# A two-layer graph network on one Trainium2 core: gathers ahead of a norm's root, means in place, one row by TensorE, two updates later

## The chip, the core and the metric

The kernel runs on one core of a Trainium2 chip. A core has five engines with an instruction queue each: TensorE (PE: matrix products and transposes; PEld is its weight load), VectorE (DVE), ScalarE (ACT), GpSimd (POOL) and SyncE (SP), which issues transfers. Sixteen DMA engines move the data. Each queue runs in its own order, and an instruction whose operands aren't ready holds up everything behind it on its engine. The metric is the device time of one execution in microseconds (us), as the median of several runs.

## The reference

There are 16 graphs of 1024 nodes with 256 features each, and one adjacency shared by all of them. Two layers are computed, each added to its input:

```python
def _gat(inp, adj_mask, W, a):
    h = jnp.matmul(inp, W)
    f1 = jnp.matmul(h, a[:F_, 0])
    f2 = jnp.matmul(h, a[F_:, 0])
    e = jax.nn.leaky_relu(f1[:, :, None] + f2[:, None, :], ALPHA)
    if adj_mask is not None:
        e = jnp.where(adj_mask[None, :, :] > 0, e, NEG_INF)
    att = jax.nn.softmax(e, axis=2)
    return jax.nn.elu(jnp.einsum('bij,bjf->bif', att, h))
...
h = jnp.maximum(_layernorm(x, axis=-1), 0.0)
out = jax.nn.relu(jnp.matmul(h, mlp1_w) + mlp1_b)       # 256 -> 512
out = jax.nn.elu(_gat(out, None, W_fc, a_fc)) + out     # dense attention
out = jax.nn.relu(jnp.matmul(out, mlp2_w) + mlp2_b)     # 512 -> 256
out = jax.nn.elu(_gat(out, adj, W_hand, a_hand)) + out  # masked attention
x = x + jax.nn.relu(out)
h = jnp.maximum(_layernorm(x, axis=-1), 0.0)
x = x + <masked attention of h with W, a, slope 0.01, relu in place of elu>
```

## The kernel before

**Tiles and stages.** A graph's nodes are cut into 8 tiles of 128 (two halves of four). For each graph the kernel goes through these stages: the first norm (`Norm`, name `0`), mlp1, dense attention (`Dense`), mlp2, the first masked attention (`Gnn0`, tensors `hma`, `atta`, `oa`), the second norm (`Norm`, name `1`), the second masked attention (`Gnn1`, `hmb`, `attb`, `ob`) and the store. The stages of neighbouring graphs are interleaved, so that a graph's masked attentions run while the next graph's dense attention is prepared.

**Dense attention without a dense product.** A softmax weight of the dense attention depends on a node only through one number. The kernel therefore ranks the nodes by that number (`rank`, L516 to L523), scatters their rows in sorted order to a table in memory (`scatter`, L530), reads the table back (`read_sorted`, L574), and forms running sums from both ends (`sum_before`, `sum_behind`, L602 to L617). It writes these to a fine table (sums within blocks of 8 rows, L609) and a coarse one (sums over blocks, `carry`, L631). `sign` (L553, on ScalarE, one pass over 1024 numbers for each tile) counts each node's place; `gather` (L642, GpSimd) fetches the fine row at that place and then adds the coarse one; `share` (L654 to L657, VectorE) works out the denominators, and `mean` (L664 on ScalarE, L666 on VectorE) makes a tile's mean, called `hp`. `merge` (L713 to L717) transposes four `hp` tiles and takes the elu; `merge_end` (L723 on VectorE, L724 on GpSimd) adds it to `resT`, which mlp2 (L731) reads.

**Graph 0 is different.** It is `split`: its first half goes through a plain product (`weight`, `product`, `product_mean`, L687 to L706), while only its second half goes through the tables. Its gathered tiles have the tag `hm`. An `hp` tile has a pool of four buffers, shared by the halves.

**The order of the work.** It is written out by hand. `at(lo, hi, steps)` puts steps into a table with due times in nominal microseconds. The table is sorted by due time, and each step issues its instructions in that order onto all queues that it uses. For TensorE, VectorE, ScalarE and SP this order is binding; on GpSimd it is enforced with dependencies, with scatters free among themselves. Due times only make an order: an engine runs ahead or behind as its operands allow. Graph b's own base is at `b * 142 - 28` (0 for graph 0), and the opening is counted from `START = -168`. A due time of -61.2 in the opening comes at about 122 us of the trace, and 0 at about 184.

**The masked attentions.** `row` needs one number of each node along the free axis, in all partitions. For graphs in `AHEAD` (1 to 14) `send` transposes the numbers, copies them and writes them to memory from ScalarE's queue (L243 to L246), and `row(True)` reads them back to all partitions from SP's queue (L360). For graphs 0 and 15 `row()` makes eight transposes of a broadcast column on TensorE (L238) and two copies on ScalarE (L365). `weight` (L375) then makes an `att` tile on VectorE, in a ring of 8 buffers, and `product` (L385) uses it. `finish`, `combine` (ScalarE, then two adds on GpSimd, L413 and L414) and `update` (L418, VectorE) end a tile; `stats` (L262, L263) and `root` (L267, L268, GpSimd) prepare the second norm; `center` (L272) and `turn` (L282) transpose it for the next projection.

Around the update, GpSimd's order in a steady graph is: adds of tiles 4 and 5, four fine gathers of the next graph's first half, the norm's first root, adds of tiles 6 and 7, four more fine gathers, two coarse ones, the norm's second root, the other coarse ones.

Of the kernel before, what the change touches and what calls it, by code (L numbers as in the profile page):

```python
# [8 lines left out]
F32 = mybir.dt.float32  # L9
# [8 lines left out]
P = 128  # L18
# [13 lines left out]
def fast_path(ctx: ExitStack, tc: tile.TileContext, alarm, x, adj, w1, b1, w2, b2, w_fc, a_fc,  # L32
# [24 lines left out]
    NT = N // P  # L57
# [3 lines left out]
    TH = HALF // P  # L61
    R = H + 2
    K = H + 1
# [3 lines left out]
    work = ctx.enter_context(tc.tile_pool(name="work", bufs=2))  # L67
# [154 lines left out]
    def at(lo, hi, steps):  # L222
        for i, step in enumerate(steps):
            table.append((lo + (hi - lo) * i / len(steps), len(table), step))
# [212 lines left out]
    class Dense:  # L437
# [221 lines left out]
        def mean(self, h, u):  # L659
            n = TH // len(self.got[h])  # L660
            got, den = self.got[h][u // n][:, u % n, :], self.dens[h]
            name = f"{self.b}_{h}_{u}"
            part = work.tile([P, K], F32, tag="part", name=f"part_{name}")
            nc.scalar.activation(part, got[:, :K], AF.Copy, scale=den[:, 1, u:u + 1])  # L664
            hp = self.hps[h, u] = work.tile([P, K], F32, tag="hp", name=f"hp_{name}", bufs=TH)
            nc.vector.scalar_tensor_tensor(hp, got[:, K:], den[:, 0, u:u + 1], part,  # L666
                                           op0=OP.mult, op1=OP.add)

# [86 lines left out]
    xs = {}  # L755
# [17 lines left out]
    def each(f, *ranges):  # L773
        out = [()]
        for r in ranges:
            out = [o + (i,) for o in out for i in r]
        return [partial(f, *o) for o in out]

    def first_norm(t0, b):

        n = norm1[b]
        lo = t0 - (62 if b == 2 else 33.5)
        at(lo, lo + 1, n.stats_steps(0))
        at(t0 - 13, t0 - 9, n.stats_steps(1))
        n.turn_at(t0 - (14.5 if b == 2 else 22), 0, 4 if b == 2 else 7)
        n.turn_at(t0 + 0.2, 1, 4)
# [49 lines left out]
    def gathers(d, h, lo, hi):  # L836
        at(lo, lo + 4, each(d.gather, [h], [0], range(TH)))
        at(hi, hi + 7, each(d.gather, [h], [1], range(TH)))
# [20 lines left out]
    def merges(lo, d, h):  # L859
        at(lo, lo + 9.2, each(d.merge, [h], range(HC)))  # L860
        at(lo + 2.5, lo + 11.7, each(d.merge_end, [h], range(HC)))

    def second_mlp(t0, b, after=0):
        d, m = dense[b], gnn0[b]
        for i, lo in enumerate((102.5, 104.8, 113, 116.5)):
            lo += t0 - 3.4 * last(b)
            at(lo, lo, [partial(d.mlp2, i // FC, i % FC)])
        t0 += after
        at(t0 + 135, t0 + 142, each(m.project, range(NT)))
        at(t0 + 141.9, t0 + 141.9, [m.extremes])  # L870

    def weights(m, t, n, lo, hi):
        at(lo, hi, each(m.weight, [t], [n], range(NT)))

    def masked_first(t0, b):
        m, n = gnn0[b], norm2[b]
        at(t0 + 1, t0 + 1, [m.vectors])
        lo = t0 + 11
        if b in AHEAD:
            at(t0 + 3.4, t0 + 3.4, [m.send])  # L880
            at(t0 + 6, t0 + 6, [partial(m.row, True)])
            lo += 7
        else:
            at(t0 + 4, t0 + 4, [m.row])
        at(t0 + 4.5, lo - 1, each(m.scale, range(NT)))
        weights(m, 0, 2, lo - 5.5, lo - 1)
        at(t0 + 10, t0 + 10, [partial(load_again, b)])
        if last(b, 2):
            for q, start in enumerate((0.5, 2, 4.2, 5.5)):
                at(t0 + start, t0 + start, [partial(dense[b].natural, q)])  # L890
        else:
            at(t0 + 4.5, t0 + 11, each(dense[b].natural, range(NT // 2)))
        pairs = [(t, 2) for t in range(0, NT, 2)]
        if last(b):
            pairs[-1:] = [(NT - 2, 1), (NT - 1, 1)]
        for t, n_t in pairs:
            start = lo + 3.5 * t
            at(start, start + 3.5 * n_t, each(m.product, [t], [n_t], range(NT)))
            if t:
                weights(m, t, n_t, start - 5.5, start + 1)  # L900
        for t in range(NT):
            end = lo + 7.2 + 7 * (t // 2) + 0.6 * (t % 2)
            if last(b) and t == NT - 2:
                end -= 3.5
            at(end, end, [partial(m.finish, t)])
            at(end + 1.2, end + 1.2, [lambda t=t: m.combine(t, dense[b].o_nat)])
            if last(b) and t >= NT - 2:
                at(end + 2.6, end + 2.6, [lambda t=t: m.add(t, dense[b].o_nat, nc.vector)])
                end -= 2
            at(end + 5.2, end + 5.2, [lambda t=t: m.update(t, xs[b])])  # L910
            end += 5.6 if last(b) else 6.2 if b == 0 else 9
            at(end, end, [partial(n.stats, t)])
        at(lo + 25 - 3.4 * last(b), lo + 25 - 3.4 * last(b), [partial(n.root, 0)])
        lo += 33.1 if last(b) else 35.5 if b == 0 else 38.5
        at(lo, lo, [partial(n.root, 1)])

    def last(b, n=1):
        return b >= NB - n
# [58 lines left out]
    AHEAD = range(1, NB - 1)  # L977
# [4 lines left out]
    START = -168.0  # L982
    n, d = norm1[0], dense[0]
# [34 lines left out]
    for t in range(TH):  # L1018
        lo = START + 95 + 7.1 * t
        at(lo, lo + 7, each(d.product, [t], range(NT)))  # L1020
        at(lo + 8.2, lo + 8.2, [partial(d.product_mean, t)])
    at(START + 100, START + 107, each(d.weight, [1], range(NT)))
    gathers(d, 1, START + 108, START + 114)
    e = dense[1]
    at(START + 95.5, START + 95.5, [e.columns])
    at(START + 98.5, START + 98.5, [e.row, e.highest])
    at(START + 99, START + 118, each(e.rank, range(NT)))
    at(START + 118, START + 118, [less_columns])
    merges(START + 125, d, 0)
    at(START + 135, START + 135, [partial(d.share, 1)])  # L1030
    at(START + 135.5, START + 137, each(d.mean, [1], range(TH)))
    merges(START + 138.2, d, 1)
    second_mlp(START + 39, 0, -13)
    at(START + 123.4, START + 141, each(e.project, range(NT), [0]))
    scatters(e, START + 126, START + 142)
# [1 line left out]
    at(START + 142.5, START + 142.5, [e.read_sorted])  # L1037
    at(START + 76, START + 76, [partial(load_first, 2)])
    first_norm(0, 2)
    at(START + 147, START + 147, [e.sums_begin])  # L1040
    at(START + 144, START + 158, each(e.sign, range(NT)))
    for h in range(2):
        at(START + 150 + 3 * h, START + 150 + 3 * h, [partial(e.sums_weights, h)])
        at(START + 151 + 5 * h, START + 156 + 5 * h, each(e.sum_before, tiles(h)))
# [6 lines left out]
    for b in range(NB):  # L1051
        base, after_base = base_of(b), base_of(b + 1)
        masked_first(base, b)
        second_norm(base, b)
        pairs = range(0, NT, 2)
# [25 lines left out]
        if b + 3 < NB:  # L1081
            lo = after_base - PERIOD + 86
            at(lo, lo, [partial(load_first, b + 3)])
            first_norm(after_base, b + 3)
# [433 lines left out]
def two_layer_gat(tc, *args):  # L1518
    nc = tc.nc
    with tc.tile_pool(name="alarm", bufs=1) as pool:  # L1520
        alarm = pool.tile([1, 1], I32, name="alarm")
        fast_path(tc, alarm, *args)
        with tc.If(nc.values_load(alarm[0:1, 0:1], min_val=0, max_val=1,
                                  skip_runtime_bounds_check_because="it is 0 or 1") > 0):
            general_path(tc, *args)
# [24 lines left out]
```

## Time and profile before

| | us |
|---|---|
| median of 3 runs (lowest, highest) | 2355.42 (2349.34, 2355.79) |
| the profiled execution | 2359.75 |
| its span, first to last instruction | 2357.9 |
| TensorE busy | 2268.6 (96%) |
| VectorE busy | 1625.7 (69%) |
| ScalarE busy | 1241.3 (53%) |
| GpSimd busy | 951.4 (40%) |
| GpSimd idle before L267 (root), waiting for VectorE | 148.4, 48.0 of it at once |
| VectorE idle before L418 (update), waiting for GpSimd | 55.5, in 14 waits |
| VectorE idle before L375, waiting for the row's transfer | 11.5, in 10 waits |

A timeline line has the start, the duration, the engine, the source line, the operation, what it writes and reads, its shape and count, and in brackets the engine's idle time before it with the instruction that ended it. A group of lines that follow one another is merged. The number of a wait says what an engine lost; whether the kernel lost it too depends on what stood behind.

### The profile page before, as it was taken

The numbers are of one execution on the slowest core, as the hardware profiler recorded it, in microseconds if no ns is written. First come the engines' busy times: TensorE is split into PE (matmuls) and PEld (weight loads), VectorE is DVE, ScalarE is ACT, GpSimd is POOL, SyncE is SP. The second block draws the span as 40 slices with busy tenths as digits, with TensorE's granted clock in tenths as the row PEclk, the third lists the DMA queues.
The fourth block names the chain that finished last, engine by engine and source line by source line (L and its number), as shares of the span: only waits on it lengthen the run. The fifth ranks groups of instructions, "written<-read, shape, count | busy, mean of one in ns | idle before, by whom it ended". The sixth has DMA issues, their size and how long they took to land. (4 is left out here: it accounts for less than half of the span.)

```text
span 2357.9 us, 30868 instructions
## 1 busy us (share of the span) xinstructions
PE 2268.6 (96%) x9955; PEld 1747.4 (74%) x9955; DVE 1625.7 (69%) x4535; ACT 1241.3 (53%) x2744; POOL 951.4 (40%) x1212
## 2 busy tenths in 40 slices
PE   8989999999999999999999999999999999999888
PEld 6667787777878778786776877777786876877666
DVE  6666685866858567685866867576685856767655
ACT  5345655647365463745546374554736546373442
POOL 1153435354443536334263543526444353533420
PEclk9999999999999999999999999999999999999999
DMA  4658366572656747366573745657265673737500
GB/s 173 165 159 210 72 176 165 167 193 97 200 118 175 180 143 184 97 187 161 172 187 113 186 115 165 174 161 181 91 195 143 174 184 125 185 95 182 140 21 27
DMA packets 150874, 355.81 MB, mean 151 GB/s; under 512 B 11224, under 2 KB 62760, under 8 KB 146608
## 3 DMA queue, kind: packets, MB, share of 16 engines
q1 hardware_dynamic: 104080, 189.58, 28.8%
q0 software_dynamic: 45952, 163.99, 26.3%
q8 instruction: 82, 1.34, 0.2%
q14 instruction: 88, 0.72, 0.1%
q10 hardware_dynamic: 672, 0.17, 0.0%
HBM read 227.40 MB, written 126.30 MB: 150 GB/s over the span
## 5 line engine op out<-in xcount | busy, mean ns | idle before, releaser
L385 PE MATMUL ob<-hmb,attb 128*128 128x257 f32 x2048 | 467.9, 386 | 21.4 <-DVE attb L375 17.0
L470 PE MATMUL h<-wfc_sb,resT 128*128 128x257 f32 x2048 | 465.7, 380 | 0.0
L385 PE MATMUL oa<-hma,atta 128*128 128x258 f32 x2048 | 454.7, 381 | 7.2 <-DVE atta L375 7.1
L385 PEld LDWEIGHTS ob<-hmb,attb 128*128 128x128 f32 x2048 | 387.2, 192 | 88.1 <-DVE attb L375 21.0
L385 PEld LDWEIGHTS oa<-hma,atta 128*128 128x128 f32 x2048 | 387.6, 190 | 67.0 <-issue 5.1
L470 PEld LDWEIGHTS h<-wfc_sb,resT 128*128 128x128 f32 x2048 | 379.5, 190 | 53.5 <-issue 0.7
L724 POOL TENSOR_TENSOR resT<-resT,e 128x512 f32<-128x512 f32 x128 | 163.6, 1278 | 371.4 <-DVE e L723 330.1
L375 DVE SCALAR_TENSOR_TENSOR atta<-rowsa,qwda,edge 128x256 f32<-128x256 f32 (+1 forms) x520 | 268.4, 545 | 27.6 <-PE oa L385 12.8
L413 POOL TENSOR_TENSOR posa<-posa,onat 128x256 f32<-128x256 f32 x118 | 98.7, 836 | 461.8 <-ACT posa L401 461.6
L375 DVE SCALAR_TENSOR_TENSOR attb<-rowsb,qwdb,edge 128x256 f32<-128x256 f32 (+1 forms) x536 | 247.9, 503 | 8.9 <-PE ob L385 5.5
L427 ACT ACTIVATE rb<-ob,recb 128x256 f32<-128x256 f32 x128 | 59.0, 475 | 346.1 <-DVE recb L425 329.4
L456 PE MATMUL m<-hT,w_sb 128*128 128x512 f32 x512 | 235.0, 598 | 0.5 <-ACT posa L401 0.5
L731 PE MATMUL m<-resT,w_sb 128*128 128x512 f32 x512 | 230.3, 596 | 4.3 <-POOL resT L724 4.3
L642 POOL DMA_INDIRECT got<-coarse,k x124 | 200.7, 1618 | 38.9 <-issue 37.7
L400 ACT ACTIVATE ea<-oa,reca 128x256 f32<-128x256 f32 x128 | 60.7, 474 | 271.2 <-DVE reca L397 262.1
L715 DVE TENSOR_SCALAR e<-hpT 128x512 f32<-128x512 f32 x128 | 88.3, 690 | 134.3 <-PE hpT L713 101.4
L731 PEld LDWEIGHTS m<-resT,w_sb 128*128 128x128 f32 x512 | 93.9, 191 | 106.3 <-issue 90.9
L456 PEld LDWEIGHTS m<-hT,w_sb 128*128 128x128 f32 x512 | 92.6, 193 | 95.9 <-issue 91.7
L642 POOL DMA_INDIRECT got<-fine,k x124 | 125.7, 1013 | 74.4 <-DMA fine<-xs 41.9
L530 POOL DMA_INDIRECT sorted<-hnat,place x128 | 131.9, 1030 | 39.6 <-issue 20.5
L553 ACT ACTIVATE junk<-r,fs 128x1024 int8<-128x1024 f32 x124 | 142.4, 1149 | 8.7 <-POOL fs L474 5.3
L716 ACT ACTIVATE e<-e 128x512 f32<-128x512 f32 x128 | 80.7, 631 | 84.2 <-DVE e L715 84.1
(186 smaller groups left out, 3445.8 us busy)
## 6 DMA issues: line engine op xcount, KB each, us to landing
xs<-sorted SPq DMA_DIRECT2D x32, 1028.0 KB
fine<-tt SPq DMA_DIRECT2D x32, 1026.0 KB
fine<-xs SPq DMA_DIRECT2D x32, 1026.0 KB
x<-in_x_dram SPq DMA_DIRECT2D x16, 1024.0 KB
xn<-in_x_dram SPq DMA_DIRECT2D x15, 1024.0 KB
out_dram<-x SPq DMA_DIRECT2D x28, 512.0 KB
coarse<-carry SPq DMA_DIRECT2D x32, 256.5 KB
r<-row_r SPq DMA_DIRECT2D x14, 512.0 KB
```

The costliest lines, as they stand in the source:

```text
L375: nc.vector.scalar_tensor_tensor(a_t[:, :n * P], self.rows[:, i], self.qwd[:, 1, j:j + 1], edge[:, j, i], op0=OP.max, op1=OP.mult)
L385: nc.tensor.matmul(self.out[t][:, :F + self.ONES], lhsT=self.att[t0, j][:, (t - t0) * P:(t - t0 + 1) * P], rhs=self.hm[:, j, 2:2 + F + sel ...
L413: adder.tensor_add(pos, pos, o_nat[:, t, :])
L456: nc.tensor.matmul(ps, lhsT=w1_sb[:, kc, c * P:(c + 1) * P], rhs=hT[:, kc, h * HALF:(h + 1) * HALF], start=(kc == 0), stop=(kc == FC - 1))
L470: nc.tensor.matmul(ps[:, :F + 1], lhsT=self.resT[:, kc, t * P:(t + 1) * P], rhs=wfc_sb[:, kc, g, :], start=(kc == 0), stop=(kc == HC - 1))
L530: made = nc.gpsimd.indirect_dma_start(out=sorted_d[self.b % 2], out_offset=bass.IndirectOffsetOnAxis(ap=self.place[:, t:t + 1], axis=0), i ...
L553: nc.scalar.activation(junk, self.r2, AF.Sign, bias=self.fs[:, 0, t:t + 1], accum_out=self.signs[:, t:t + 1])
L642: nc.gpsimd.indirect_dma_start(out=got[u // n][:, u % n, :], out_offset=None, in_=(coarse_d if coarse else fine_d)[self.b % 2][:, :], in_o ...
L715: nc.vector.tensor_scalar_min(e, ps, 0.0)
L716: nc.scalar.activation(e, e, AF.Exp)
L724: nc.gpsimd.tensor_add(dst, dst, e)
L731: nc.tensor.matmul(ps, lhsT=w2_sb[:, kc, c * P:(c + 1) * P], rhs=self.resT[:, kc, h * HALF:(h + 1) * HALF], start=(kc == 0), stop=(kc == H ...
```

## The change

Five edits, made together:

1. In `mean`, graph 0's second half writes each mean over the second part of the gathered sums, and takes no `hp` tile.
2. Graph 2's first-half statistics and the root after them go from 62 to 49 before its base. The gathers of graph 0's second half go from START + 108 and + 114 to START + 101 and + 106. With that, the gathers stand ahead of the root on GpSimd.
3. In the opening, `product_mean` is due 0.6 earlier, `share(1)` at 130 instead of 135, the means from 130.5 to 135 instead of 135.5 to 137, the second half's merges at 136 instead of 138.2, and graph 1's `sign` steps from 130 to 150 instead of 144 to 158.
4. Graph 14's first row is made by TensorE; `send` and the transfer are left out for it. The start of its products stays where it was.
5. For tiles 6 and 7 of graphs 1 to 14, `update` is due 1.5 later.

```diff
-            hp = self.hps[h, u] = work.tile([P, K], F32, tag="hp", name=f"hp_{name}", bufs=TH)
+            hp = self.hps[h, u] = got[:, K:] if self.split else work.tile(
+                [P, K], F32, tag="hp", name=f"hp_{name}", bufs=TH)
...
-        lo = t0 - (62 if b == 2 else 33.5)
+        lo = t0 - (49 if b == 2 else 33.5)
...
         if b in AHEAD:
+            lo += 7
+        if b in AHEAD and not last(b, 2):
             at(t0 + 3.4, t0 + 3.4, [m.send])
             at(t0 + 6, t0 + 6, [partial(m.row, True)])
-            lo += 7
         else:
             at(t0 + 4, t0 + 4, [m.row])
...
-            at(end + 5.2, end + 5.2, [lambda t=t: m.update(t, xs[b])])
+            updated = end + (6.7 if t >= NT - 2 and b in AHEAD else 5.2)
+            at(updated, updated, [lambda t=t: m.update(t, xs[b])])
...
-        at(lo + 8.2, lo + 8.2, [partial(d.product_mean, t)])
+        at(lo + 7.6, lo + 7.6, [partial(d.product_mean, t)])
...
-    gathers(d, 1, START + 108, START + 114)
+    gathers(d, 1, START + 101, START + 106)
...
-    at(START + 135, START + 135, [partial(d.share, 1)])
-    at(START + 135.5, START + 137, each(d.mean, [1], range(TH)))
-    merges(START + 138.2, d, 1)
+    at(START + 130, START + 130, [partial(d.share, 1)])
+    at(START + 130.5, START + 135, each(d.mean, [1], range(TH)))
+    merges(START + 136, d, 1)
...
-    at(START + 144, START + 158, each(e.sign, range(NT)))
+    at(START + 130, START + 150, each(e.sign, range(NT)))
```

## The prediction

> **What bounds the kernel now.** I read the page first, then TensorE's timeline for its gaps, then the engine that each gap names, over the same stretch.
>
> The page's first section, busy time by engine:
>
> ```profile
> PE 2268.6 (96%) x9955; PEld 1747.4 (74%) x9955; DVE 1625.7 (69%) x4535; ACT 1241.3 (53%) x2744; POOL 951.4 (40%) x1212
> ```
>
> TensorE is the bound, with 89 us idle. All that the change can win is in that idle time, and in the half-speed clock after it. TensorE's timeline, in the opening, around graph 4's update, late in graph 7 and at graph 14's first product (start, us, group, idle before it):
>
> ```profile
> 124.80 2.01 PE L695 MATMUL od<-hnat,attd 128*128 128x257 f32 x8 [1.55 <-ACT hpd L705]
> ...
> 150.01 0.30 PE L713 MATMUL hpT<-ident,hp 128*128 128x128 f32 x1 [1.57 <-DVE hp L666]
> ...
> 152.65 0.33 PE L713 MATMUL hpT<-ident,hp 128*128 128x128 f32 x1 [1.73 <-DVE hp L666]
> ...
> 167.91 1.13 PE L731 MATMUL m<-resT,w_sb 128*128 128x512 f32 x2 [1.14 <-POOL resT L724]
> 169.95 2.03 PE L731 MATMUL m<-resT,w_sb 128*128 128x512 f32 x2 [0.92 <-POOL resT L724]
> ...
> 780.27 4.55 PE L385 MATMUL ob<-hmb,attb 128*128 128x257 f32 x12 [3.55 <-DVE attb L375]
> ...
> 1209.95 1.43 PE L282 MATMUL nt<-ident,hn 128*128 128x128 f32 x8 [0.42 <-DVE hn L272]
> ...
> 2136.94 14.59 PE L385 MATMUL oa<-hma,atta 128*128 128x258 f32 x64 [2.44 <-DVE atta L375]
> ```
>
> The opening loses 1.55 us to a late mean, some 4 to late means of the second half (hp), and 2 to GpSimd's resT. In the steady graphs TensorE stalls at the second norm's transpose (nt): 0.42 in most graphs. GpSimd's and VectorE's timelines say why, opening and graph 7:
>
> ```profile
> 122.24 0.23 POOL L267 TENSOR_SCALAR rstd<-mv 128x4 f32<-128x4 f32 x1 [48.03 <-DVE mv L263]
> ...
> 123.79 1.11 POOL L642 DMA_INDIRECT got<-fine,k  x1 [0.20 <-issue]
> ...
> 1193.15 1.04 POOL L642 DMA_INDIRECT got<-fine,k  x1 [0.30 <-issue]
> 1194.21 0.26 POOL L267 TENSOR_SCALAR rstd<-mv 128x4 f32<-128x4 f32 x1
> ```
> ```profile
> 1192.53 1.64 DVE L375 SCALAR_TENSOR_TENSOR attb<-rowsb,qwdb,edge 128x256 f32<-128x256 f32 x4
> 1197.14 0.93 DVE L418 SCALAR_TENSOR_TENSOR x<-ea,x 128x256 f32<-128x256 f32 x1 [2.97 <-POOL ea L414]
> ```
>
> From 1189.36 to 1209.35 GpSimd works without a real pause: four gathers, a root, four adds, four gathers, two more, the second root. nt comes 0.60 after that root's end in graphs 1 to 3, 5 to 9 and 11 to 13 alike. So a steady graph is bound by GpSimd's chain for 20 us, and VectorE's 2.97 wait for ea lies under it.
>
> **What the Trainium skill says.** "TensorE: Matmul & The Clock Gate", section "What's actually happening": after an idle window of about 3.4 us the array gets half its clock for the next. The trace agrees: matmuls from 781.0 to 784.4 start 0.43 us apart instead of 0.217, at clock 0.50. Two such windows lie in the opening (153 to 156.4, 170 to 173.4). "SBUF — State Buffer", section "Who interferes with whom": a VectorE instruction with two SBUF inputs excludes a GpSimd one that reads SBUF. The trace agrees: a mean's hp takes 0.75 us, and 1.93 beside GpSimd's resT. "DMA: Bandwidth & Descriptors", section "Issuing engines are not separate DMA queues": all transfers share 16 engines; DMA's busy share is 1.02 to 1.13 at 102 to 106 us.
>
> **The change part by part.**
>
> *Gathers and stats, opening.* The root due at -61.2 and the four statistics at -62 go behind the gathers, to -48. In VectorE's queue the four pairs (0.42+0.18 us, 2.2 in sum) leave the place ahead of rank 4 and product_mean 1. That mean falls from 124.02 to 121.8, its ScalarE part ends at 122.5, TensorE's product 2 ends at 123.25: the 1.55 wait goes. The statistics land behind product_mean 2, where VectorE idled 2.05 (131.4 to 133.5): they cost nothing there; without that cover 2.2. The 0.6 earlier due time of the means passes one weight at most: nothing. The gathers, held by the root till 123.79, now wait only for their tables. The semaphores say fine landed at 119.1, coarse at 120.2 and 121.2. So they start some 3.5 earlier (2.6 to 4.6), and the last coarse gather lands at about 141 instead of 144.5. GpSimd's copies for graph 1's projections no longer queue behind them.
>
> *Means and signs.* Until here TensorE runs 1.55 ahead: projection 0 at 132.1, third transposes at 138.9. VectorE's new order is min 2, end 1, share, mean 0, mean 1, min 3, end 2, mean 2, mean 3, end 3. Share starts at 140.8 and, met by GpSimd's resT as before (1.85 for one operation), ends by 143.2. ScalarE's order is exp 2 (to 141.6), projection copy, sign 0 (1.25), parts 0 and 1 (0.67 each: 144.5), exp 3, copy, sign 1, parts 2 and 3. Min 3 waits for mean 1, ends at 146.0; exp 3 to 147.3, copy 147.6, sign 1 148.9, parts to 150.2; mean 3 starts at 150.3, transpose at 151.1 against 153.3. Before, seven projections were done by then, now six (1.74 us): the lead shrinks to 0.5 us. It returns behind: the signs (8 of 1.27) are no longer ahead of the last exp at 165.2, so end 3 of the second half ends at 163.9 instead of 168.4, resT at 165.8 instead of 169.9, and the two mlp2 waits (2.06) and the second half-speed window (1.7) go. Adding up to mlp2's end: projections 2 x 1.74, transposes 3 x 0.44, mlp2 4 x 3.45, nt 0.9 from 151.3, 0.7 for a half-speed stretch after the 4.5 us stall: 171.5 against 176.9, so 5.4 earlier; a second half-speed window costs 1.7, weighed half. ScalarE's next wait, for sorted rows (landed 166.3 and 168.8), moves little, since scatter 7 still follows the last projection; it ends before mlp2's last output. I take **-4.2** (both ends: -6 to -1). In place of hp tiles the gathered tiles live longer, but their buffers are next wanted at graph 0's projection, 11 us after the last transpose: nothing.
>
> *Graph 14's row.* Removed: a transpose, a copy (0.24), ScalarE's and SP's DMA. Added, from graph 0's row: 8 transposes in 1.04 us and two copies, 1.07. SP's, VectorE's and GpSimd's timelines of graph 14:
>
> ```profile
> 2131.80 0.32 SPq L360 DMA_DIRECT2D rowsa<-row_a  x1
> 2132.17 0.43 SPq L86 DMA_DIRECT2D x<-in_x_dram  x1
> 2132.72 8.04 SPq L609 DMA_DIRECT2D fine<-tt  x2
> ```
> ```profile
> 2136.31 0.48 DVE L375 SCALAR_TENSOR_TENSOR atta<-rowsa,qwda,edge 128x256 f32<-128x256 f32 x1 [3.02 <-DMA rowsa<-row_a]
> ```
> ```profile
> 2173.22 0.99 POOL L642 DMA_INDIRECT got<-fine,k  x1 [3.67 <-DMA fine<-xs]
> ```
>
> The first weight goes from 2136.31 to 2133.3, behind the sums. TensorE is free at 2134.5 plus 0.75 for the transposes: 2135.25 instead of 2136.94, -1.7. Behind SP's row stood the x load, and behind that the table writes; each megabyte of these lands 7 to 10 us after the one before (2148.0, 2157.8, 2165.1, 2172.5). Without the row's half megabyte, and with x issued at 2125.8, I estimate the last 4 to 5 us earlier. The gather then waits for the adds (2169.54 less 1.7) instead: at best 5.2 is won. If landings don't move further than their issue, 1.7. I take **-4.6**, near the upper end, since the landings form one backlog.
>
> *Updates.* Graphs 1 to 14, tiles 6 and 7: in VectorE's order two weights pass update 6, and recip and a center pass update 7. TensorE gets weights 6 and 7 early, but weight 0 of the next pair stays behind both updates, 0.7 earlier only. And nt stays tied to GpSimd: the 3.55 of graph 4 and its half-speed window cost just 0.37 at nt (0.97 instead of 0.60 after the root), likewise graph 10: -0.7. Against it, VectorE's stream now runs 0.8 longer, into the root. In eight graphs (1, 3, 5, 7 to 9, 11, 13) the root starts 0.05 us after that stream's last weight (1194.17, 1194.21), and the gather before it takes 1.04 instead of 0.94, as if already held. If held for both weights, 8 x 0.8 = 6.4 later; if it slips between, nothing; I take 0.33 each: +2.6. Together **+1.9** (-0.7 to +5.7).
>
> Sum: -4.2 - 4.6 + 1.9 = -6.9. The profiled execution took 2359.75 (span 2357.9 and 1.85 around it), 4.3 over the median; taken off its own time, 2352.9; off the median 2355.4, **2348.5**, my forecast.
>
> **Rivals.**
> 1. The toll on GpSimd is nil: -9.5, 2346. For: 0.26 us operations slip in elsewhere. Against: the eight coincidences.
> 2. Only one of the two gains arrives (row limited to 1.7, or ScalarE's signs delay the parts further): -2 to -4, about 2352.5. For: the lead of 0.5 at 151.
> 3. Slower: the toll alone. Roots wait out both weights and later GpSimd work collides too: 0.8 x 14 = 11, with the opening giving 1 and the row 1.7: about 2364. It decides against the change from 0.6 us a graph (8.8/14); 1.2 would be needed to lose 0.3% beside full gains. For: the chain has no slack. Against: only eight graphs are timed so.
> 4. No change: the opening's stall before the transposes grows, share waiting at VectorE's head for a coarse gather landing as late as 144.5 (+3.5), cancelling its gain and part of the row's: 2355.
>
> **How the numbers follow.** 0.3% is 7.1 us, about what measurement can tell from no change. Forecast 0.42 (2345 to 2352, faster in half of it), rival 1 0.22 (faster), rival 2 0.18 (mostly same), rival 4 0.09, slower 0.09. Faster 0.45, same 0.45, slower 0.10. The range, 2341 to 2358, takes in rivals 1, 2 and 4.
>
> **What would show it.** Right: no wait at product 3; the first gather at 119 to 122; hpT's stall near 146 to 151; no wait for resT; pa (L322) at 171 to 173. In graph 14 the first weight at its sums' end, gather without a landing wait. Root 1 tied to nt at 0.60 still, with the first root 0.3 later. Wrong: share idle for DMA past 142, a root on time, the landing of fine less than 2 us earlier, or a graph's length changed elsewhere.

## The result and the profile after

The changed kernel took 2365.66 us (median of 5 runs, 2360.86 to 2367.26) beside 2355.42 (median of 5, 2349.34 to 2355.79) for the kernel before: a ratio of 1.0046, 95% interval 1.0030 to 1.0063. It is slower by 10.2 us, where 2348.5 was forecast in a range that ended at 2358. The two profiled executions hide this: 2360.86 after is the fastest of its five and had the highest granted clock (0.996, the others 0.992 or 0.993), and 2359.75 before was above all five of the kernel before. What the traces show in each stage is therefore of more use than their ends.

The page's busy line of the changed kernel:

```profile
PE 2264.1 (96%) x9962; PEld 1746.9 (74%) x9962; DVE 1625.8 (69%) x4535; ACT 1243.4 (53%) x2745; POOL 955.8 (41%) x1212
```

TensorE has no more to do than before. GpSimd is busy 4.4 us longer with as many instructions: some of them became slower. TensorE's timeline of the changed kernel, at the places that the prediction showed (start, us, group, idle before it):

```profile
118.72 7.33 PE L696 MATMUL od<-hnat,attd 128*128 128x257 f32 x33
...
147.69 0.41 PE L714 MATMUL hpT<-ident,got 128*128 128x128 f32 x2 [1.74 <-issue]
...
151.26 0.33 PE L714 MATMUL hpT<-ident,got 128*128 128x128 f32 x1 [3.17 <-DVE got L667]
...
161.78 7.03 PE L732 MATMUL m<-resT,w_sb 128*128 128x512 f32 x16
...
782.10 1.10 PE L385 MATMUL ob<-hmb,attb 128*128 128x257 f32 x4 [0.50 <-DVE attb L375]
...
1214.57 1.41 PE L282 MATMUL nt<-ident,hn 128*128 128x128 f32 x8 [1.44 <-DVE hn L272]
...
2141.45 0.82 PE L385 MATMUL oa<-hma,atta 128*128 128x258 f32 x3
```

In the opening the wait at the product (1.55) and those for resT (2.06) are gone, and the second half-speed window with them; the two late means cost 4.9 in sum. Graph 14's first product waits for nothing (2.44 before). In graph 4 the wait for a weight fell from 3.55 to 0.50. But the wait at nt grew from 0.42 to 1.44. Five rows of GpSimd's timeline in graph 7 say what stands behind it:

```profile
1193.59 1.00 POOL L642 DMA_INDIRECT got<-fine,k  x1 [0.16 <-issue]
...
1198.45 0.44 POOL L267 TENSOR_SCALAR rstd<-mv 128x4 f32<-128x4 f32 x1
1198.97 1.14 POOL L268 TENSOR_TENSOR rstd<-rstd,power 128x4 f32<-128x4 f32 x1
...
1203.33 1.27 POOL L642 DMA_INDIRECT got<-fine,k  x1 [0.17 <-PE ob L385]
1204.91 1.33 POOL L642 DMA_INDIRECT got<-fine,k  x1 [0.31 <-issue]
```

The fifth and sixth gather of that graph in the kernel before:

```profile
1198.82 1.08 POOL L642 DMA_INDIRECT got<-fine,k  x1 [0.16 <-issue]
1200.21 1.00 POOL L642 DMA_INDIRECT got<-fine,k  x1 [0.31 <-issue]
```

And VectorE's timeline after, with the last line's counterpart from before below it:

```profile
1196.77 2.43 DVE L375 SCALAR_TENSOR_TENSOR attb<-rowsb,qwdb,edge 128x256 f32<-128x256 f32 x6
1201.65 0.93 DVE L418 SCALAR_TENSOR_TENSOR x<-ea,x 128x256 f32<-128x256 f32 x1 [2.45 <-POOL ea L414]
...
1227.35 0.16 DVE L654 TENSOR_TENSOR den<-got,qd 128x4 f32<-128x4 f32 x1 [3.71 <-DMA got<-coarse,k]
```
```profile
1221.33 0.16 DVE L654 TENSOR_TENSOR den<-got,qd 128x4 f32<-128x4 f32 x1 [2.30 <-DMA got<-coarse,k]
```

The stream of weights is six long instead of four and runs over the root, which takes 0.44 instead of 0.26; its second instruction takes 1.14 (1.05). The first two of the second four gathers take 1.27 and 1.33 (1.08 and 1.00). VectorE's wait for ea shrank from 2.97 to 2.45, and nt still comes 0.60 after the second root. The share was in no part of the prediction's account of the updates: the first share of the next graph waits 3.71 for a coarse gather to land, 2.30 before. TensorE then waits for the means (hp) at hpT: in the stretch from 240 to 2030 us, 14.7 us in 40 waits, where it was 6.5 in 19.

Counted at stage starts, the changed kernel stands 5.0 us ahead at graph 0's masked attention (172.96 against 176.90, though its trace was 1.04 behind when the opening's changed part began), loses 10.7 in the steady graphs up to graph 14, and wins 4.4 there. Two of the three terms are near their forecasts; the third is not.

Summed over graphs 1 to 13, the 10.7 has a clear place. The fifth gather comes 2.2 us later after the first than before, the second root 1.4 later after the fifth gather, and the first share 13.1 later after the second root; TensorE's shorter waits for weights (attb, 12.0 before and 5.9 after) take part of that back. In this trace only the seven odd graphs meet the root with weights (0.42 to 0.44 for the root); in the even ones the gathers wait 0.8 to 2.8 for their tables, and the root comes after the weights, at 0.25.

### The profile page after: what moved, and what is told of

Same layout as the page of the kernel before. It is cut to its first block, busy times and chain, and to the rows that moved or that the text cites. A ratio compares the mean times of both kernels' runs of the same rounds, so it can differ in the third digit from the quotient of the medians.

```text
span 2359.1 us, 30884 instructions
## 1 busy us (share of the span) xinstructions
PE 2264.1 (96%) x9962; PEld 1746.9 (74%) x9962; DVE 1625.8 (69%) x4535; ACT 1243.4 (53%) x2745; POOL 955.8 (41%) x1212
## 5 line engine op out<-in xcount | busy, mean ns | idle before, releaser
L385 PE MATMUL ob<-hmb,attb 128*128 128x257 f32 x2048 | 459.0, 382 | 12.0 <-DVE attb L375 8.5
L375 DVE SCALAR_TENSOR_TENSOR attb<-rowsb,qwdb,edge 128x256 f32<-128x256 f32 (+1 forms) x536 | 239.5, 493 | 8.9 <-PE ob L385 5.5
L642 POOL DMA_INDIRECT got<-fine,k x124 | 131.3, 1059 | 117.0 <-DMA coarse<-carry 45.6
```

The source lines that it names most:

```text
L375: nc.vector.scalar_tensor_tensor(a_t[:, :n * P], self.rows[:, i], self.qwd[:, 1, j:j + 1], edge[:, j, i], op0=OP.max, op1=OP.mult)
L385: nc.tensor.matmul(self.out[t][:, :F + self.ONES], lhsT=self.att[t0, j][:, (t - t0) * P:(t - t0 + 1) * P], rhs=self.hm[:, j, 2:2 + F + sel ...
L642: nc.gpsimd.indirect_dma_start(out=got[u // n][:, u % n, :], out_offset=None, in_=(coarse_d if coarse else fine_d)[self.b % 2][:, :], in_o ...
```

## The experiments

The theories at the start: **A**, the later updates cost the steady graphs their time; **C**, the opening's new order leaves something behind in the graphs after it; **D**, the traces differ by the run's own variation. Each experiment is timed beside the kernel before on its own chip (5 or 8), where that took 2341.7 to 2343.6. Ratios are to it, with 95% intervals; the difference of two ratios is known to 3 or 4 us.

**1. The change in three parts.** The updates alone (graphs 1 to 14, as in the change):

```diff
-            at(end + 5.2, end + 5.2, [lambda t=t: m.update(t, xs[b])])
+            updated = end + (6.7 if t >= NT - 2 and b in AHEAD else 5.2)
+            at(updated, updated, [lambda t=t: m.update(t, xs[b])])
```

> The kernel before with the third part alone: the updates of tiles 6 and 7 due 1.5 us later in graphs 1 to 13. Theory A (this part costs the steady graphs their time: the two traces lose about 10.7 us between the end of graph 0's products and graph 14): +9 to +13 us, a ratio of about 1.0045. Theory C (the opening's new order leaves something behind in the graphs after it): within 3 us of the kernel before. Theory D (the difference of the traces is the run's own variation): within 3 us as well. The prediction's own term was +1.9.

Measured: 2362.23, ratio 1.0089 (1.0076 to 1.0102): +20.8.

Everything but the updates, that is, in the changed kernel:

```diff
-            updated = end + (6.7 if t >= NT - 2 and b in AHEAD else 5.2)
-            at(updated, updated, [lambda t=t: m.update(t, xs[b])])
+            at(end + 5.2, end + 5.2, [lambda t=t: m.update(t, xs[b])])
```

> The changed kernel with tiles 6 and 7 updated when they were before, so the opening's new order and graph 14's row by TensorE alone. Theory A: the traces' gains stay, -5.0 for the opening and -4.4 for the row, so -7 to -10 us, about 2347; it would beat both kernels. Theory C: about as slow as the changed kernel, +3 to +10. The prediction's terms give -8.8.

Measured: 2335.08, ratio 0.9970 (0.9961 to 0.9978): -7.0.

The row alone:

```diff
         if b in AHEAD:
+            lo += 7
+        if b in AHEAD and not last(b, 2):
             at(t0 + 3.4, t0 + 3.4, [m.send])
             at(t0 + 6, t0 + 6, [partial(m.row, True)])
-            lo += 7
```

> The kernel before with graph 14's row by TensorE alone. The prediction's term is -4.6 (between -5.2 and -1.7), the traces' reading -4.4; theory D: 0.

Measured: 2339.19, ratio 0.9988 (0.9981 to 0.9994): -2.8.

The opening's edits alone (the change's diff without the hunks of row and updates):

> The kernel before with the opening's edits alone (gathers ahead of the third graph's root, means over the gathered sums, earlier due times of means, share, merges and signs). The prediction's term is -4.2 (between -6 and -1), the traces' reading at the end of the opening -5.0. Theory C: the opening's gain is given back in the steady graphs, so 0 to +8.

Measured: 2337.85, ratio 0.9983 (0.9977 to 0.9990): -4.0.

The parts add up: -2.8 and -4.0 make -6.8, and 0.9970 x 1.0089 = 1.0059, inside the interval of the whole change. C and D fall. The updates alone make the change slow, and by nearly twice what A had read off the traces. In these runs the steady graphs hardly wait for tables, so one graph is like the next, and two traces can be laid side by side. Graph 7 on TensorE and VectorE, without the updates:

```profile
1191.80 1.10 PE L385 MATMUL ob<-hmb,attb 128*128 128x257 f32 x4 [0.32 <-DVE attb L375]
1200.43 1.41 PE L282 MATMUL nt<-ident,hn 128*128 128x128 f32 x8 [0.42 <-DVE hn L272]
1216.42 0.33 PE L714 MATMUL hpT<-ident,hp 128*128 128x128 f32 x1 [0.30 <-DVE hp L667]
```
```profile
1211.83 0.16 DVE L654 TENSOR_TENSOR den<-got,qd 128x4 f32<-128x4 f32 x1 [2.33 <-DMA got<-coarse,k]
```

and with the updates alone:

```profile
1215.17 1.43 PE L282 MATMUL nt<-ident,hn 128*128 128x128 f32 x8 [1.44 <-DVE hn L272]
1231.18 0.33 PE L713 MATMUL hpT<-ident,hp 128*128 128x128 f32 x1 [0.27 <-DVE hp L666]
1232.06 0.33 PE L713 MATMUL hpT<-ident,hp 128*128 128x128 f32 x1 [0.56 <-DVE hp L666]
1232.72 0.33 PE L713 MATMUL hpT<-ident,hp 128*128 128x128 f32 x1 [0.33 <-DVE hp L666]
```
```profile
1228.14 0.16 DVE L654 TENSOR_TENSOR den<-got,qd 128x4 f32<-128x4 f32 x1 [3.88 <-DMA got<-coarse,k]
```

The wait at the weight is gone, nt's is 1.02 longer, share starts 12.97 after nt instead of 11.40, and three waits follow it at hpT. From 240 to 2030 us, TensorE's waits before nt grow from 5.3 to 17.1, those before hpT from 6.4 to 14.7, and those for attb fall from 3.0 to nothing. The trace of the updates alone also has two half-speed windows of 3.41 us in that stretch, at 950.8 and 1937.3, which the one without them doesn't have. The prediction had half speed follow an idle window of about 3.4 us; in the 3.41 us before these two TensorE was idle for only 1.30 and 1.72, so here less was enough. Half speed carries part of the loss: over all runs the median granted clock is 0.993 with the updates alone and 0.995 for the kernel before beside it, which is worth at most about 5 us of the 20.8 (an estimate: 0.002 of 2362).

**2. Which update, and what stands between.** Two ways are left within A: **A1**, GpSimd's chain is late, by the root that the weights hold, and all that hangs on it is late with it; **A2**, it is what VectorE does beside the second four gathers. And a third comes from SP's timeline. Without the updates, and with them alone (two transfers merged in a line; the start is the store's):

```profile
1193.60 10.59 SPq L434 DMA_DIRECT2D out_dram<-x  x2
```
```profile
1207.31 11.64 SPq L434 DMA_DIRECT2D out_dram<-x  x2
```

The fifth gather of these graphs starts at 1189.31 and at 1203.94, so the store of half a megabyte is issued 4.29 and 3.37 us after it. It waits for the second layer's update of tile 3 of the graph before, which stands behind updates 6 and 7 in VectorE's order, and VectorE gets there sooner. **S**: that store goes among the packets of the fine gathers and makes the coarse ones late.

Only tile 6 later, in the changed kernel:

```diff
-            updated = end + (6.7 if t >= NT - 2 and b in AHEAD else 5.2)
+            updated = end + (6.7 if t == NT - 2 and b in AHEAD else 5.2)
```

> Opening and row as in the change; of the updates only tile 6's is later, so that two weights pass it and VectorE's weights run on beside GpSimd's first root, while tile 7's update stays where it was. Theory A1 (the root held by the weights, 0.27 us a graph, and all that hangs on GpSimd's chain): the gathers after the root start 0.26 later, the first share's wait for its coarse gather grows by about 1.1, and the loss against opening and row alone is +15 to +20 (a ratio to before of 1.003 to 1.006). Theory A2 (it is what VectorE does beside the second four gathers): the root's 0.27 alone, +3 to +4 against opening and row alone, so a ratio of about 0.9985.

Measured: 2338.05, ratio 0.9983 (0.9973 to 0.9993), +3.0 against opening and row alone, hardly more than the noise of two ratios.

Only tile 7 later, the same with `t == NT - 1`:

```diff
-            updated = end + (6.7 if t >= NT - 2 and b in AHEAD else 5.2)
+            updated = end + (6.7 if t == NT - 1 and b in AHEAD else 5.2)
```

> Opening and row as in the change; of the updates only tile 7's is later, so that a reciprocal and a center pass it. Theory A1: the root isn't met, so 0 to +3 against opening and row alone (ratio 0.997 to 0.9983). Theory A2: the gathers of the second four are lengthened (1.08 to 1.27, 1.00 to 1.33), the coarse gathers land later, and most of the loss, +10 to +16, is here (ratio 1.001 to 1.004).

Measured: 2334.62, ratio 0.9974 (0.9966 to 0.9983), the same as without it.

Tile 6 alone meets the root and makes GpSimd's chain 0.30 us a graph late (0.38 with both), and costs little; tile 7 alone lengthens no gather and costs nothing. A1 falls, and A2 in the form given: the 17 us need both. With one update left in place VectorE still stops for ea 6 or ea 7 and the store comes at 4.47 and 4.29; only with both later do the two weights fill a wait, and the store moves to 3.37.

The store held back in the changed kernel, with the update that it waits for:

```diff
-                at(end + 1.5 + 0.6 * u, end + 1.5 + 0.6 * u, [lambda t=t + u: m.update(t, xs[b])])
+                lo = end + 1.5 + 0.6 * u + 0.6 * (t + u == TH - 1 and not last(b, 2))
+                at(lo, lo, [lambda t=t + u: m.update(t, xs[b])])
```

> The changed kernel, with the last update of the second layer's tile 3 later in VectorE's order (behind tile 7's statistics and a weight), so that the store that waits for it is issued 4.3 us after the fifth gather's start, as before the change, in place of 3.4. Theory S (the store comes earlier and gets in the way of the fine gathers, and this makes the coarse ones land late): the share's wait falls by 0.6 to 1.1 us a graph, -8 to -14 against the changed kernel. Theories A1 and A2: within 3 us of the changed kernel, about 1.004 against before.

Measured: 2347.70, ratio 1.0025 (1.0015 to 1.0034). Against 1.0059 for the parts' product, that is -8, the low end of what S named, and the share comes 0.65 earlier a graph. About half of the loss stays, which S doesn't explain.

GpSimd made late by itself, with VectorE's order untouched (one memset of 256 elements had no room in its pool and gave no time, so there are two of 16):

```diff
+    def idle():
+        nc.gpsimd.memset(small.tile([P, 16], F32, tag="idle", name="idle", bufs=1), 0.0)
...
+        at(t0 + 48.2, t0 + 48.2, [idle] * 2)
         at(t0 + 48.5, t0 + 53, fine[4:])
```

> Opening and row as in the change, the updates where they were, and two small GpSimd memsets (estimated 0.3 us in sum) between the last adds and the second four gathers of graphs 2 to 14. VectorE's order, and with it the store, stays as before. Theory A1 (GpSimd's lateness alone makes the coarse gathers land late): the first share's wait grows by about 1 us a graph, +10 to +20 against opening and row alone. Theory S (the early store does that): the lateness goes through one to one, nt and share each 0.3 later, +2 to +5, a ratio of about 0.9985.

Measured: 2345.09, ratio 1.0012 (1.0004 to 1.0020), +9.8 against opening and row alone. The dose was larger than meant: the memsets take 0.11 each, but the fifth gather started 0.66 later. Of the 9.8, 0.61 x 13 = 7.9 is that lateness at the second root, one to one; the share came another 0.33 later. And since the gather came later, the store stood 3.63 after it instead of 4.29. So this run decides nothing alone; but 0.61 late on GpSimd costs less here than 0.38 together with what else the updates do.

**3. One store.** The cause taken away, not shifted:

```diff
-            elif t % TH + n == TH:
-                at(end + 2.8, end + 2.8, [lambda t=t: m.store(t // TH * TH, TH, xs[b], b)])
+            elif t + n == NT:
+                at(end + 2.8, end + 2.8, [lambda: m.store(0, NT, xs[b], b)])
```

With opening and row alone, then with the whole change:

> Opening and row as in the change, the updates where they were, and in graphs 0 to 13 one store of 1 MB after the last tile in place of two of half a megabyte, so that none is issued amid the fine gathers. Theory S: the fine gathers and the first coarse ones have the DMA engines for themselves, the fourth coarse gather is done 0.8 to 1.3 us earlier after the fifth gather, TensorE's waits for hp (6.4 us in sum) go: -4 to -7 against opening and row alone, a ratio of about 0.9945. Otherwise (the landings hang on the gathers' issue): 0, ratio 0.997.

Measured: 2325.09, ratio 0.9932 (0.9918 to 0.9945). That is -9 against opening and row with two stores (through the ratios, since the chips differ), more than expected; the waits for hp give 5.1 of it (9.6 to 4.5). The rest isn't explained: in the traces TensorE's busy time is 4.2 shorter as well (2255.1 against 2259.3).

> The changed kernel, updates later included, with the same one store. Theory S: what is left of the update edit's loss is GpSimd's chain, about 0.36 us a graph, +5 against opening and row with one store, so about 5 to 8 under the kernel before, a ratio of 0.996 to 0.998. Otherwise: most of the loss stays, ratio 1.003 or more.

Measured: 2330.10, ratio 0.9954 (0.9940 to 0.9967): slower by 5.0 than the same without the updates (each of its five runs is slower than each of the other's), where the updates had cost 17 to 20 with two stores. The first share of graph 7, with one store, without the updates and with them:

```profile
1204.85 0.16 DVE L654 TENSOR_TENSOR den<-got,qd 128x4 f32<-128x4 f32 x1 [2.14 <-DMA got<-coarse,k]
```
```profile
1208.65 0.16 DVE L654 TENSOR_TENSOR den<-got,qd 128x4 f32<-128x4 f32 x1 [1.58 <-DMA got<-coarse,k]
```

The waits before hpT over the whole execution, without the updates and with them, both with one store:

```profile
  DVE hp L667: 4.5, 11
```
```profile
  DVE hp L667: 4.3, 10
```

What the updates had cost at hpT (8.3) is gone. What they leave is at nt, again over the whole execution:

```profile
  DVE hn L272: 25.1, 21
```
```profile
  DVE hn L272: 37.6, 22
```

The 12.5 more at nt is mostly time that TensorE now waits here in place of earlier, since the weights come sooner; the net is GpSimd's chain, 0.38 a graph, 4.9 in 13 graphs.

**4. Is the early store enough?** Only the second layer's update of tile 3, earlier:

```diff
-                at(end + 1.5 + 0.6 * u, end + 1.5 + 0.6 * u, [lambda t=t + u: m.update(t, xs[b])])
+                lo = end + 1.5 + 0.6 * u - 0.5 * (t + u == TH - 1 and not last(b, 2))
+                at(lo, lo, [lambda t=t + u: m.update(t, xs[b])])
```

> Opening and row as in the change, the updates where they were, and only the last second-layer update of tile 3 earlier in VectorE's order (ahead of a weight and of one tile's statistics), so that the first store of graphs 0 to 12 is issued about 3.35 us after the fifth gather's start, as in the changed kernel, in place of 4.3, and nothing on GpSimd moves. If the early store alone is enough: the first share's wait grows by 0.9 to 1.1 us a graph, +12 to +15 against opening and row alone, a ratio of 1.002 to 1.0035. If it takes the early store together with the lengthened gathers: 0 to +6, a ratio of 0.997 to 0.9995.

Measured: 2335.40, ratio 0.9969 (0.9955 to 0.9983): no loss. S in its plain form falls as well: the store has to meet the lengthened gathers. The table has the steady graphs of all these traces (medians over graphs 1 to 13, the share's column their mean; us; the rows "before" and "change" are from the two profiles of the result, the others from the experiments). Lateness of a graph is what the columns "fifth gather", "second root" and "share" gain over the second row; "measured" is the difference of the ratios times 2341.9.

| kernel | fifth gather after first | fifth, sixth gather take | store after fifth gather | second root's end after fifth gather | first share after that | sum x 13 | measured |
|---|---|---|---|---|---|---|---|
| before | 9.47 | 1.08, 1.01 | 4.29 | 10.53 | 12.46 | | |
| opening and row | 9.46 | 1.08, 1.00 | 4.29 | 10.53 | 12.38 | 0 | 0 |
| tile 6 later | 9.58 | 1.25, 1.01 | 4.47 | 10.71 | 12.46 | +4.9 | +3.0 |
| tile 7 later | 9.46 | 1.08, 1.00 | 4.29 | 10.53 | 12.36 | -0.3 | +0.9 |
| early store | 9.47 | 1.08, 1.01 | 3.37 | 10.83 | 12.27 | +2.6 | -0.2 |
| GpSimd late | 10.12 | 1.15, 1.06 | 3.63 | 10.48 | 12.71 | +12.2 | +9.8 |
| change, store held | 9.74 | 1.27, 1.33 | 4.29 | 10.64 | 12.89 | +11.7 | +12.9 |
| change | 9.73 | 1.27, 1.33 | 3.37 | 10.64 | 13.47 | +19.1 | (+17) |
| updates alone | 9.73 | 1.27, 1.33 | 3.37 | 10.63 | 13.54 | +19.9 | +20.8 to before |
| one store | 9.46 | 1.08, 1.01 | 14.5 | 10.54 | 11.68 | | |
| change, one store | 9.74 | 1.27, 1.33 | 14.6 | 10.64 | 11.63 | +4.3 to one store | +5.0 |

(The bracketed 17 is 10.2 plus 6.8, from two measurements.) The share comes 1.1 late where the gathers are lengthened and the store goes among them: 0.5 with the store at its old place, none without a store, and none with the early store beside a fifth and sixth gather of the old length (its seventh takes 1.46 instead of 1.12, and the second root is 0.3 later for it). In the trace's DMA packets, the second four fine gathers take 7.3 us of the 16 engines in the updates alone and 6.9 without; with one store 7.3 and 6.8. So the longer gathers cost half a microsecond of DMA time anyway. Only where a half-megabyte store is also issued among them does the share come late. From the second root on the DMA engines are full (a mean busy share of 1.07 without the updates and 1.06 with them, 0.76 before it), so a backlog that can't be made up is the likely way; that this is how the delay reaches the share is argued, not shown. Why the packets take longer, and what of VectorE's work lengthens those two gathers, I could not settle.

**5. The chain shortened.** If GpSimd's chain sets the pace, work taken off it pays. To opening, row and one store:

```diff
-                self.add(t, o_nat, nc.vector if self.beside_gathers else nc.gpsimd)
+                beside = self.beside_gathers or t == NT - 2 and self.b in AHEAD
+                self.add(t, o_nat, nc.vector if beside else nc.gpsimd)
```

> Opening and row, the updates where they were, one store, and tile 6's two adds in graphs 1 to 13 on VectorE in place of GpSimd. The theory that GpSimd's chain from the first root to the second sets nt: the second four gathers start up to 1.5 us earlier, TensorE's wait before nt (5.3 us in sum) and the one for the last pair's first weight (3.0) go, and it gains 4 to 8 beside one store alone, a ratio of about 0.992. If VectorE becomes the bound in its place (its stream is 0.8 to 1.9 us longer there): 0 or a loss.

Measured: 2310.67, ratio 0.9871 (0.9856 to 0.9886): 14.4 less than with one store alone, more than expected, and the fastest kernel here. In the two traces TensorE's idle time falls by 9.8 (66.7 to 56.9) and its busy time by 4.5, which isn't explained. VectorE's timeline in one graph shows the adds in what had been its wait, at 0.43 us each, and update 6 without a wait:

```profile
1172.01 0.43 DVE L414 TENSOR_TENSOR posa<-posa,onat 128x256 f32<-128x256 f32 x1 [0.90 <-ACT posa L401]
1173.59 0.43 DVE L415 TENSOR_TENSOR ea<-ea,posa 128x256 f32<-128x256 f32 x1 [1.15 <-ACT ea L407]
...
1178.30 0.41 DVE L419 SCALAR_TENSOR_TENSOR x<-ea,x 128x256 f32<-128x256 f32 x1
```

On GpSimd the fifth gather now comes 8.16 after the first (9.46), and the weights meet this root too (0.36):

```profile
1169.71 1.00 POOL L643 DMA_INDIRECT got<-fine,k  x1 [0.16 <-issue]
...
1174.53 0.36 POOL L267 TENSOR_SCALAR rstd<-mv 128x4 f32<-128x4 f32 x1
...
1177.87 1.08 POOL L643 DMA_INDIRECT got<-fine,k  x1 [0.16 <-issue]
```

TensorE's total before nt falls to this, in fewer waits; none of them lies between 240 and 2030 us:

```profile
  DVE hn L272: 18.8, 8
```

## Why the prediction failed

**The opening, -4.2: right.** -4.0 by itself, -5.0 in the trace. (Its own sum, 5.4 less half of 1.7, gives 4.5, not 4.2.) The steps held: no wait at product 3, first gather at 120.50 (119 to 122 forecast), hpT's stall at 147 to 151, no wait for resT, pa at 172.96 (171 to 173). Share didn't wait past 142 for the coarse landing, as rival 4 had it: it began at 141.55.

**Graph 14's row, -4.6: right in mechanism, its size hangs on the tables' landing.** It was split into 1.7 at TensorE and the rest from tables that land earlier. In the trace of the changed kernel both came: no wait at the first product (2.44 before), and 1.72 instead of 3.67 for the table, 4.4 in sum. The wait for the table was to go altogether, and 1.72 of it stayed. By itself the row gave 2.8. On that chip the gather doesn't wait for the table even with the old row (opening alone):

```profile
2146.44 0.99 POOL L642 DMA_INDIRECT got<-fine,k  x1 [0.16 <-issue]
```

and only the TensorE part (2.45 at the first product there) can be won. Both numbers lie between the prediction's 1.7 and 5.2.

**The updates, +1.9: wrong; 17 to 21.** The step that failed is "Together +1.9 (-0.7 to +5.7)". Its two terms came out near what was forecast; the third, which the step put at nothing, is most of the loss.
- The toll on the root was about right. It was put at 0.33 in eight graphs, 2.6; in the changed kernel's trace it is 0.28 at the root in seven graphs and 0.10 at what follows in all thirteen, 3.3 in sum. Where no graph waits for its tables, as in the experiments, all thirteen meet the root: 4.9, beside the 5.0 that the updates cost with one store.
- The gain of 0.7 in graphs 4 and 10 came at nt, which follows the second root by 0.60 there too, instead of 0.97. It is small beside the rest.
- The largest term was put at nothing. I followed VectorE's earlier stream to the weights and stopped. The store on SP that waits for a later instruction of the same stream went unfollowed, and so did the gathers lengthened beside it. Their meeting makes the next graph's first share 1.0 to 1.2 us late, 12 us after the second root, 13 to 15 us over 13 graphs, and TensorE pays for it at hpT. The prediction's test list did name "a graph's length changed elsewhere" as what would prove it wrong.

**Rival 3** named 2364 with lost gains and 0.8 us a graph. The time is close by luck, the way to it is not the one that happened: the gains arrived, and the root's toll is about a quarter of the loss.

Two statements of the Trainium skill bear on this. "SBUF — State Buffer", section "Who interferes with whom", has a VectorE instruction with two SBUF inputs contend with a GpSimd one that reads SBUF; the trace agrees, since a weight has two SBUF inputs, and the root beside two weights takes 0.44 instead of 0.26. "DMA: Bandwidth & Descriptors", section "Issuing engines are not separate DMA queues", was cited for the opening and bears on the missed term as well: SP's store and GpSimd's gathers share the 16 engines, and with one store the loss at the share is gone.

## What to carry to other kernels

When an instruction moves back in one engine's order, everything behind it comes earlier: list the transfers that wait for those instructions, and see what they meet on the DMA engines when issued earlier. A chain without slack on a little-used engine (GpSimd at 40%) is paid for in every iteration; work taken off it went with a gain of 14 us (with one store), where giving its neighbour more freedom lost 17. Where two causes are suspected, try each alone and both: here neither the early store nor one late update cost more than 3 us.

## What the runs showed of the hardware

- With one store of 1 MB in place of two of 0.5 MB, issued behind four coarse gathers instead of amid the fine ones, the ratio went from 0.9970 to 0.9932, about 9 us. Nothing waits for these stores. Of the 9, 5.1 are TensorE's waits for hp.
- Two memsets of 0.11 us on GpSimd moved the gather behind them by 0.66 us a graph.
- The kernel before took 2355.42 in the result's measurement and 2341.7 to 2343.6 in the experiments. In the first trace, six of the even graphs' first gathers waited 0.87 to 3.84 us for the tables to land, 14.4 in sum; in the traces of the opening alone and of the updates alone no such wait in a steady graph is over 0.4. A term that counts on a landing (the row's) was worth 4.4 in the one and 2.8 in the others. The record names the chip of the experiments but not the first one, so whether the chip makes the difference isn't known.
